# A GNN and LSTM kernel on one core: the first layer's split reordered, one DRAM tensor per tile of gate inputs, an early activation, and the fc weight one tile sooner

## The chip, the cores and the metric

The kernel runs on one core of a Trainium2 chip. Five engines work side by side: TensorE (PE, with its weight loads PEld), VectorE (DVE), ScalarE (ACT), GpSimd (POOL) and SyncE (SP), which here only issues transfers. Each takes its own instructions in order and waits on semaphores for the others. The metric is the device time of one execution, in microseconds; lower is better. Three runs of the kernel before gave 1154.37, 1154.40 and 1155.09 us, median 1154.4.

## What is computed

`x` is 1250 x 512 float32. First comes a graph network on the layer norm of x, then an LSTM over the 1250 rows as one sequence, each added to its input:

```
h    = layernorm(x) @ fc_w.T + fc_b
norm = clip(degree(dst), 1) ** -0.5
layer(v, l): agg = segment_sum((v * norm)[src], dst) * norm
             f, f0 = 0.9 * agg, 0.1 * h
             relu((1-b)*f + b*(f @ w1) + (1-b)*f0 + b*(f0 @ w2) + bias)    b = log(1/l + 1)
x2  = x + layer(layer(h, 1), 2)
out = x2 + lstm(layernorm(x2))     # gates f, i, o: sigmoid; candidate: tanh; hidden size 512
```

There are 20000 edges.

## The kernel before

The rows are cut into 10 tiles (T) of 128 rows. Tile t holds steps 4t to 4t+3 of each of 32 stretches (P) of 40 steps (LEN), because the LSTM is later run on all 32 stretches at once, each started 90 steps early (WARM), instead of one row after the other. A test at the end compares neighbouring stretches and falls back to one row at a time (L862) if they are apart.

**Start (L273 to L486).** Loads are issued on SyncE's queue in program order: source nodes, two tiles of x (`load_rows(0, 2, xt)`, two transfers a tile), the fc weight (L291), tiles 2 and 3, the fc bias (L295), tiles 4 to 9 in eight transfers (L125), then the two w2 weights and two biases. VectorE turns the edges into one-hot rows (`make_onehot`, L373 and L375) and computes layer norm statistics (`stats`, L152) and scales (`scales`, with a square root on ScalarE, L88). ScalarE applies them (`normed`, L401). PE multiplies one-hots into the adjacency `adj` (L389), and the normed tiles with the fc weight into `h` (L175, added at L460), and `h` with the two w2 weights (L175), which VectorE adds to the bias as `base` (`add_base`, L440). In this part the order on PE, VectorE and ScalarE is written out by hand (`manual_schedule`, L310): each of the three runs its instructions as the program lists them, in 13 slots (L442).

**The split.** The aggregation is done in bf16 with each value as a sum of three bf16 planes. For each tile `split_first` does: ScalarE writes plane 0 as h times norm in bf16 (L251), VectorE writes the remainder (`rest`, L253, two buffers), ScalarE rounds it to plane 1 (L256), VectorE writes what is left as plane 2 (L259). Tiles go in the order 6, 7, 8, 9, 0, 1, 2, 3, 4, 5. Three are split in slot 10, three in slot 11, four after the last slot, and after them come the adds of tiles 8 and 9.

**The branch (L897).** The number of edges that are missing from `adj` (L227) is read by every engine, and `fast` or `general` is taken. With these inputs it is `fast`. There the order of instructions is chosen by the planner, which sees what each one waits for, and not by the program's order; an instruction inside the branch stays inside.

**The layers (L703).** PE aggregates for four blocks of 128 features (L722): for each tile k in the order above, three planes times three groups of columns, nine matmuls. Then come products with w1 (L175), and VectorE and ScalarE finish the layer; at the end of the second, `rstd_of` (L88 again) scales groups of tiles.

**The gate inputs (L888).** For each tile PE multiplies with the input weights (L550), VectorE and ScalarE split the sum into three planes (`put_planes`, L765 and L236 to L239), and SyncE stores them to the DRAM tensor `xp_d` (L893). Early steps of the first stretch are zeroed by one transfer from POOL (L752).

**The LSTM (L796).** 130 steps. SyncE loads a step's planes (L771, five buffers), PE adds them into PSUM (L572) and multiplies the state with the weights (L580), then a chain of ScalarE and VectorE forms the new state (L587 to L598). PE, VectorE and ScalarE are hand-ordered again (L827).

Of the kernel before, what the change touches and what calls it, by code (L numbers as in the profile page):

```python
# [38 lines left out]
def gnn_lstm_kernel(  # L39
# [23 lines left out]
    nc = tc.nc  # L63
# [49 lines left out]
    def load_rows(i0, i1, dst):  # L113


        for p0, p1 in ((0, 16), (16, P - 1)):
            if i1 - i0 <= 4:
                for i in range(i0, i1):
                    nc.sync.dma_start(
                        dst[4 * p0:4 * p1, i, :],  # L120
                        bass.AP(tensor=x.tensor, offset=x.offset + (LEN * p0 + 4 * i) * D,
                                ap=[[LEN * D, p1 - p0], [D, 4], [1, D]]))
            else:
                for q in range(4):
                    nc.sync.dma_start(  # L125
                        dst[4 * p0 + q:4 * p1:4, i0:i1, :],
                        bass.AP(tensor=x.tensor, offset=x.offset + (LEN * p0 + 4 * i0 + q) * D,
                                ap=[[LEN * D, p1 - p0], [4 * D, i1 - i0], [1, D]]))
# [66 lines left out]
    with ExitStack() as gnn_stack:  # L195
# [48 lines left out]
        def split_first(pool, tiles):  # L244

            rest = {}
            for n in range(len(tiles) + 1):
                if n < len(tiles):
                    t = tiles[n]
                    rest[t] = pool.tile([R, D], F32, name="rest")  # L250
                    nc.scalar.activation(planes[:, t, 0, :], h[:, t, :], AF.Copy,  # L251
                                         scale=norm[:, t:t + 1])
                    nc.vector.scalar_tensor_tensor(rest[t], h[:, t, :], norm[:, t:t + 1],  # L253
                                                   planes[:, t, 0, :],
                                                   op0=OP.mult, op1=OP.subtract)
                    nc.scalar.copy(planes[:, t, 1, :], rest[t])  # L256
                if n:
                    t = tiles[n - 1]
                    nc.vector.tensor_sub(planes[:, t, 2, :], rest[t], planes[:, t, 1, :])  # L259


# [11 lines left out]
        with tc.tile_pool(name="prep", bufs=1) as prep, \  # L273
# [12 lines left out]
            xt = base1  # L286

            load_last_rows(xt, nc.scalar, fill=True)
            load_rows(0, 2, xt)
            fcw = prep.tile([128, KD, D], F32, name="fcw")  # L290
            nc.sync.dma_start(fcw, fc_w.rearrange("(a p) i -> p a i", p=128))  # L291
            biases = [prep.tile([R, D], F32, name=name) for name in ("fcb", "b1", "b2")]
            fcb, *bl = biases
            load_rows(2, 4, xt)
            nc.sync.dma_start(fcb, row_bcast(fc_b, R))  # L295
            load_rows(4, T, xt)
            w2 = []
# [12 lines left out]
            with tc.manual_schedule(engines={mybir.EngineType.PE, mybir.EngineType.DVE,  # L310
# [6 lines left out]
                def stats(t0, t1):  # L317
                    for t in range(t0, t1):
                        layernorm_stats(work, mv, t, xt[:, t, :])
# [24 lines left out]
                def neg_floor_div(v, n, name):  # L344
# [9 lines left out]
                    return q, r  # L354

                np_src, o_src = neg_floor_div(e_src, LEN, "stretch")
                stats(0, 2)
                na_src, q_src = neg_floor_div(o_src, 4, "tile")
                nc.vector.scalar_tensor_tensor(low, np_src, -4.0, q_src, op0=OP.mult, op1=OP.add)
                nc.vector.scalar_tensor_tensor(key, e_dst, float(T), na_src,  # L360
                                               op0=OP.mult, op1=OP.subtract)
                scales(0, 2)

# [78 lines left out]
                for s in range(T + 3):  # L442
                    c0, c1, c2 = per_slot[s] if s < len(per_slot) else (0, 0, 0)
                    if s < T:
                        xTs[s] = transposed(work, psT, xns.pop(s), "xT")
                    if s < 3:
                        t0, t1 = ((2, 4), (4, 7), (7, T))[s]
                        stats(t0, t1)
                        scales(t0, t1)
                    normed(s + 1)  # L450
                    if 0 <= s - 4 < T - 3:
                        add_base(s - 4)
                    count(c0)
                    if 0 <= s - 1 < T:
                        ps_h[s - 1] = product(psM, xTs.pop(s - 1), fcT)
                    count(c1)
                    if 0 <= s - 2 < T:
                        hTs[s - 2] = transposed(prep2, psT, h[:, s - 2, :], "hT")
                    if 0 <= s - 1 < T:
                        nc.vector.tensor_add(h[:, s - 1, :], ps_h.pop(s - 1), fcb)  # L460
                    count(c2)
                    if s == 2:
                        for l in range(2):
                            with_identity(w2[l], ALPHA * betas[l], ALPHA * (1.0 - betas[l]))
                    if 0 <= s - 3 < T:


                        hT = hTs.pop(s - 3)
                        ps, name = (psM, "psM") if s < T + 1 else (acc, "acc")
                        if s == T + 1:  # L470
                            total(psT.tile([128, KD, R], F32, name="psT")[:1, 0, :1])
                            split_first(prep2, order[3:6])
                        ps_b[s - 3] = [product(ps, hT, w2[0], name)]
                        if s == T:
                            most_edges()
                            count_edges(psT.tile([128, KD, R], F32, name="psT")[:, 0, :])
                            row_totals()
                            degree_norm(prep)
                        ps_b[s - 3].append(product(ps, hT, w2[1], name))
                        if s == T:  # L480
                            add_base(T - 3)
                            split_first(prep2, order[:3])
                split_first(prep2, order[6:])
                add_base(T - 2)
                add_base(T - 1)
                assert counted == n_batch and not blocks  # L486
        n_missing = nc.values_load(missing, min_val=0, max_val=E + R)

# [2 lines left out]
        xw_d = dram.tile([P * LEN, 4 * G], F32, name="xw_d")  # L491


        xp_d = dram.tile([LEN, EARLY + P, 3, 4 * G], BF16, name="xp_d")
        x2_d = dram.tile([P * LEN, D], F32, name="x2_d")

        def in_time(v, i):
# [245 lines left out]

        def tile_steps(i):

            return bass.AP(tensor=xp_d.tensor,
                           offset=xp_d.offset + (4 * i * (EARLY + P) + EARLY) * 12 * G,
                           ap=[[12 * G, P], [(EARLY + P) * 12 * G, 4], [1, 12 * G]])

        def zero_steps(rows):  # L750

            nc.gpsimd.dma_start(  # L752
                bass.AP(tensor=xp_d.tensor, offset=xp_d.offset,
                        ap=[[(EARLY + P) * 12 * G, LEN], [12 * G, EARLY], [1, 12 * G]]), rows)


        v_bufs = adj.rearrange("b a i r -> b (a i r)")[:, :8 * G].bitcast(F32).rearrange(
            "b (n g) -> b n g", g=G)
        zeros = adj.rearrange("b a i r -> b (a i r)")[:EARLY * LEN, 8 * G:20 * G]
        pl_bufs = planes.rearrange("b t i d -> b (t i d)")[:, :24 * G].rearrange(  # L760
            "b (n i g) -> b n i g", n=2, i=3)

# [5 lines left out]
        def open_step(load, ps_g, n):  # L768

            xs = load.tile([3 * P, 4, NG, 128], BF16, name="xs")  # L770
            nc.sync.dma_start(  # L771
                xs.rearrange("r j g m -> r (j g m)"),
                bass.AP(tensor=xp_d.tensor,
                        offset=xp_d.offset + (n % LEN * (EARLY + P) + EARLY + n // LEN) * 12 * G,
                        ap=[[4 * G, 3 * P], [1, 4 * G]]))
            return open_gates(ps_g, lambda j: sel, lambda j, s: xs[:, j, :, 64 * s:64 * (s + 1)])

# [18 lines left out]
        def lstm(late, Wh):  # L796
# [6 lines left out]
            with tc.tile_pool(name="state", bufs=2) as state, \  # L803
# [22 lines left out]
                stores = [8, 16, 24, 32, 38, LEN]  # L826
                with tc.manual_schedule(engines={mybir.EngineType.PE, mybir.EngineType.DVE,  # L827
                                                 mybir.EngineType.Activation}):
                    hT = [state.tile([128, 2, 32], F32, name=f"hT{s}") for s in range(2)]
                    for s in range(2):  # L830
                        nc.vector.memset(cgs[s], 0.0)
                        nc.vector.memset(hT[s], 0.0)
                    for n in range(-WARM, LEN):
                        if n == 0:
                            keep_state(snap, hT)
                        ps = open_step(load, ps_g, n)
                        add_gates(ps, hT, Wh)
# [93 lines left out]
```

## Time and profile before

| what | value |
|---|---|
| median of three runs | 1154.4 us |
| the profiled execution, its own time | 1152.8 us |
| its span | 1151.0 us |
| PE busy | 1024.6 us, 89% |
| VectorE busy | 518.4 us, 45% |
| ScalarE busy | 344.9 us, 30% |
| POOL busy | 65.7 us, 6% |
| first aggregation matmul starts at | 200.4 us |
| first LSTM step starts at | 550.2 us |

The profile is of one execution. Start times are counted from the span's start. A line such as `L722 PE` means the instructions that line 722 issued on PE; `SPq` is the queue of transfers that SyncE issues. "Issue" is time in which an engine waited for nothing that the profile shows. PEclk is the share of PE's full clock that was granted.

### The profile page before, as it was taken

How to read it: one execution, taken by the hardware profiler on the slowest of the kernel's cores; microseconds unless marked ns; L12 is line 12 of the kernel's file. 1: busy time of each engine (PE TensorE's matmuls, PEld its weight loads, DVE VectorE, ACT ScalarE, POOL GpSimd, SP SyncE). 2: the span in 40 equal slices, each digit the busy share in tenths (PEclk: the TensorE clock that was granted, in tenths of full speed). 3: DMA queues.
4: the chain of work that ended last, by engine and by line, in shares of the span. 5: the costliest groups of instructions: out<-in, count | busy, mean ns of one | idle time of the engine just before them, and what ended most of it. 6: DMA issues, size and time to landing. Idle time of an engine off the chain costs nothing.

```text
span 1151.0 us, 27480 instructions
## 1 busy us (share of the span) xinstructions
PE 1024.6 (89%) x11340; PEld 535.8 (47%) x11356; DVE 518.4 (45%) x1775; ACT 344.9 (30%) x1286; POOL 65.7 (6%) x117
## 2 busy tenths in 40 slices
PE   5999996999999999999788888888888888888884
PEld 3455552554455444444444444444444444444442
DVE  7876566003300765555344434444444434434433
ACT  2321125103300033333333333333333333333332
POOL 0000000300002270000000000000000000100111
PEclk9999998999999999999999999999999999999998
DMA  8000001700200273222632222323232232333331
GB/s 233 2 1 1 1 1 58 202 1 18 72 1 1 102 222 130 110 110 110 193 97 86 90 92 86 96 84 98 85 95 87 89 93 84 105 101 97 108 83 20
DMA packets 42363, 96.22 MB, mean 84 GB/s; under 512 B 6062, under 2 KB 21783, under 8 KB 40825
## 3 DMA queue, kind: packets, MB, share of 16 engines
q1 hardware_dynamic: 38464, 83.98, 23.5%
q0 software_dynamic: 3440, 10.16, 2.8%
q8 instruction: 92, 1.51, 0.5%
q14 instruction: 46, 0.38, 0.1%
q10 hardware_dynamic: 321, 0.19, 0.1%
HBM read 71.93 MB, written 19.76 MB: 80 GB/s over the span
## 4 chain that ended last, share of the span: by engine, by line
PE 65%; DVE 17%; ACT 10%; issue 4%; DMA 2%; SPq 1%; DVEq 0%; ACTq 0%
PE gates L580 28%; PE psM L175 13%; PE agg L722 11%; PE psM L550 10%; DVE pr L593 3%; ACT th L596 3%; DVE hT L598 3%; DVE hh L597 3%; DVE cg L594 3%; ACT cg L587 3%; ACT sg L589 2%; PE acc L389 2%; DVE od L375 1%; DVE ob L373 1%; DMA fcw<-in_L_gnn_fc_w_dram 1%
## 5 line engine op out<-in xcount | busy, mean ns | idle before, releaser
L580 PE MATMUL gates<-Wh,hT 128*32 128x256 f32 x8320 | 482.5, 383 | 75.5 <-DVE hT L598 75.5
L580 PEld LDWEIGHTS gates<-Wh,hT 128*32 128x32 f32 x8320 | 245.5, 110 | 286.4 <-DVE hT L598 152.1
L593 DVE TENSOR_TENSOR pr<-sg,cg 128x128 f32<-128x128 f32 x260 | 70.5, 271 | 223.7 <-ACT sg L589 223.5
L722 PE MATMUL agg<-adj,planes 128*128 128x512 bf16 (+1 forms) x704 | 131.6, 347 | 10.8 <-DVE x L440 9.8
L550 PE MATMUL psM<-Wx,xT 128*128 128x512 f32 x320 | 138.7, 594 | 1.5 <-ACT xT L169 1.2
L587 ACT ACTIVATE cg<-gates 128x64 f32<-128x64 f32 x260 | 58.0, 223 | 248.9 <-PE gates L580 244.8
L596 ACT ACTIVATE th<-cg 128x64 f32<-128x64 f32 x260 | 66.6, 256 | 138.8 <-DVE cg L594 138.8
L722 PEld LDWEIGHTS <-planes 128*128 128x128 bf16 x720 | 71.1, 99 | 72.2 <-DVE x L440 10.6
L597 DVE TENSOR_TENSOR hh<-so,th 128x64 f32<-128x64 f32 x260 | 58.6, 225 | 86.4 <-ACT th L596 86.4
L550 PEld LDWEIGHTS psM<-Wx,xT 128*128 128x128 f32 x320 | 60.5, 190 | 76.7 <-issue 72.8
L598 DVE STREAM_TRANSPOSE hT<-hh 128x64 f32<-128x64 f32 x260 | 63.8, 245 | 28.3 <-DVE hh L597 1.4
L589 ACT ACTIVATE sg<-gates 128x128 f32<-128x128 f32 x260 | 70.8, 272 | 0.2
L594 DVE TENSOR_TENSOR cg<-pr 128x64 f32<-128x64 f32 x260 | 58.5, 225 | 8.9
L591 ACT ACTIVATE so<-gates 128x64 f32<-128x64 f32 x260 | 60.2, 232 | 0.0
L843 POOL TENSOR_TENSOR base<-base,hh 128x128 f32<-128x128 f32 x40 | 18.2, 455 | 694.6 <-issue 534.9
L175 PE MATMUL psM<-w,hT 128*128 128x512 f32 x128 | 56.9, 596 | 0.0
L572 PE MATMUL gates<-xs,sel 96*32 96x256 bf16 x1040 | 52.5, 273 | 4.0 <-DMA xs<-xp_d 4.0
L375 DVE TENSOR_SCALAR od<-ids,key 125x820 f16<-125x820 f16 (+42 forms) x160 | 55.5, 347 | 0.0
L389 PE MATMUL acc<-od,ob 125*128 125x400 f16 (+22 forms) x360 | 47.8, 259 | 4.5 <-DVE od L375 3.0
L373 DVE TENSOR_SCALAR ob<-ids,low 125x128 f16<-125x128 f16 x160 | 39.5, 247 | 17.1 <-PE acc L389 16.9
L572 PEld LDWEIGHTS <-sel 96*32 96x32 bf16 x1040 | 30.6, 98 | 28.6 <-issue 4.8
L389 PEld LDWEIGHTS <-ob 125*128 125x128 f16 x360 | 29.5, 97 | 26.8 <-issue 10.8
(152 smaller groups left out, 675.0 us busy)
## 6 DMA issues: line engine op xcount, KB each, us to landing
xs<-xp_d SPq DMA_DIRECT2D x130, 384.0 KB, 3.2
xp_d<-planes SPq DMA_DIRECT2D x10, 1536.0 KB, 5.5
w<-in_L_gnn_w_dram SPq DMA_DIRECT2D x2, 1024.0 KB
w<-in_L_gnn_w_dram POOLq DMA_DIRECT2D x2, 1024.0 KB, 7.2
xp_d<-adj POOLq DMA_DIRECT2D x1, 1440.0 KB, 7.8
h<-in_x_dram SPq DMA_DIRECT2D x10, 128.0 KB, 2.7
base<-x SPq DMA_DIRECT2D x20, 64.0 KB, 2.2
base<-x POOLq DMA_DIRECT2D x20, 64.0 KB, 2.3
```

The source lines that it names most:

```text
L175: nc.tensor.matmul(p, lT[:, k, :], rhs[:, k, :], start=(k == 0), stop=(k == KD - 1))
L389: nc.tensor.matmul(blocks[i][:, (d0 - i * BW) * T:(d1 - i * BW) * T], ob, od[:, (d0 - lo) * T:(d1 - lo) * T], start=False, stop=last)
L550: nc.tensor.matmul(p, yT[:, k, :], Wx[:, k, j, :, :], start=(k == 0), stop=(k == KD - 1))
L580: nc.tensor.matmul(ps[s][32 * j:32 * (j + 1), :, :], hT[b // 2][:, b % 2, :], Wh[:, b, j, :, 64 * s:64 * (s + 1)], start=False, stop=(b == 3))
L587: nc.scalar.activation(cg[:, 1, :], p[:, 3, :], AF.Tanh)
L589: nc.scalar.activation(sg, p[:, 0:2, :], AF.Sigmoid)
L593: nc.vector.tensor_mul(pr, sg, cg)
L594: nc.vector.tensor_add(cg[:, 0, :], pr[:, 0, :], pr[:, 1, :])
L596: nc.scalar.activation(th, cg[:, 0, :], AF.Tanh)
L597: nc.vector.tensor_mul(hh[:, m], so, th)
L598: nc.vector.transpose(hT.rearrange("p b c -> p (b c)"), hh[:, m])
L722: nc.tensor.matmul(p[:, :n * R], planes[:, k, pl, f * 128:(f + 1) * 128], adj[:, k, t0:t0 + n, :].rearrange("b i r -> b (i r)"), start=(k ...
```

## The change

- `split_first` issues a tile's second ScalarE step (L256) after the next tile's first step on both engines, not ahead of it.
- Four tiles are split in slot 11 instead of three. In slot 12 the add of tile 8 and the split of tiles 3 and 4 come ahead of the last product in program order; then come the add of tile 9 and the split of tile 5.
- `xp_d` becomes ten DRAM tensors, one per tile of gate inputs. The zeroing becomes ten transfers of 12 rows each.
- One row tile is loaded ahead of the fc weight instead of two, and statistics and scales are grouped as 0, 1 to 3, 4 to 6, 7 to 9. The scales of tile 0 come ahead of the one-hot keys.
- An activation with Sigmoid on a constant column stands first in the LSTM's hand-ordered part.

```diff
-                    nc.scalar.copy(planes[:, t, 1, :], rest[t])
                 if n:
                     t = tiles[n - 1]
+                    nc.scalar.copy(planes[:, t, 1, :], rest[t])
                     nc.vector.tensor_sub(planes[:, t, 2, :], rest[t], planes[:, t, 1, :])
...
-            load_rows(0, 2, xt)
+            load_rows(0, 1, xt)
             fcw = prep.tile([128, KD, D], F32, name="fcw")
             nc.sync.dma_start(fcw, fc_w.rearrange("(a p) i -> p a i", p=128))
...
-            load_rows(2, 4, xt)
+            load_rows(1, 4, xt)
...
-                stats(0, 2)
+                stats(0, 1)
+                scales(0, 1)
...
-                scales(0, 2)
...
-                        t0, t1 = ((2, 4), (4, 7), (7, T))[s]
+                        t0, t1 = ((1, 4), (4, 7), (7, T))[s]
...
                             total(psT.tile([128, KD, R], F32, name="psT")[:1, 0, :1])
-                            split_first(prep2, order[3:6])
+                            split_first(prep2, order[3:7])
+                        if s == T + 2:
+                            add_base(T - 2)
+                            split_first(prep2, order[7:9])
...
-                split_first(prep2, order[6:])
-                add_base(T - 2)
                 add_base(T - 1)
+                split_first(prep2, order[9:])
...
-        xp_d = dram.tile([LEN, EARLY + P, 3, 4 * G], BF16, name="xp_d")
+        xp_d = [dram.tile([4, EARLY + P, 3, 4 * G], BF16, name=f"xp_d{i}") for i in range(T)]
...
-            nc.gpsimd.dma_start(
-                bass.AP(tensor=xp_d.tensor, offset=xp_d.offset,
-                        ap=[[(EARLY + P) * 12 * G, LEN], [12 * G, EARLY], [1, 12 * G]]), rows)
+            for i in range(T):
+                nc.gpsimd.dma_start(
+                    bass.AP(tensor=xp_d[i].tensor, offset=xp_d[i].offset,
+                            ap=[[(EARLY + P) * 12 * G, 4], [12 * G, EARLY], [1, 12 * G]]), rows)
...
-        zeros = adj.rearrange("b a i r -> b (a i r)")[:EARLY * LEN, 8 * G:20 * G]
+        zeros = adj.rearrange("b a i r -> b (a i r)")[:4 * EARLY, 8 * G:20 * G]
...
+            steps = xp_d[n % LEN // 4]
...
+                    nc.scalar.activation(warm, ones, AF.Sigmoid)
                     hT = [state.tile([128, 2, 32], F32, name=f"hT{s}") for s in range(2)]
```

More of the change, by code (lines that the diff above doesn't have):

```diff
@@ L744, in tile_steps @@
         def tile_steps(i):
-            return bass.AP(tensor=xp_d.tensor,
-                           offset=xp_d.offset + (4 * i * (EARLY + P) + EARLY) * 12 * G,
+            return bass.AP(tensor=xp_d[i].tensor, offset=xp_d[i].offset + EARLY * 12 * G,
                            ap=[[12 * G, P], [(EARLY + P) * 12 * G, 4], [1, 12 * G]])
         def zero_steps(rows):
-            nc.gpsimd.dma_start(
-                bass.AP(tensor=xp_d.tensor, offset=xp_d.offset,
-                        ap=[[(EARLY + P) * 12 * G, LEN], [12 * G, EARLY], [1, 12 * G]]), rows)
+            for i in range(T):
+                nc.gpsimd.dma_start(
+                    bass.AP(tensor=xp_d[i].tensor, offset=xp_d[i].offset,
+                            ap=[[(EARLY + P) * 12 * G, 4], [12 * G, EARLY], [1, 12 * G]]), rows)
         v_bufs = adj.rearrange("b a i r -> b (a i r)")[:, :8 * G].bitcast(F32).rearrange(
             "b (n g) -> b n g", g=G)
-        zeros = adj.rearrange("b a i r -> b (a i r)")[:EARLY * LEN, 8 * G:20 * G]
+        zeros = adj.rearrange("b a i r -> b (a i r)")[:4 * EARLY, 8 * G:20 * G]
         pl_bufs = planes.rearrange("b t i d -> b (t i d)")[:, :24 * G].rearrange(
@@ L770, in open_step @@
             xs = load.tile([3 * P, 4, NG, 128], BF16, name="xs")
+            steps = xp_d[n % LEN // 4]
             nc.sync.dma_start(
                 xs.rearrange("r j g m -> r (j g m)"),
-                bass.AP(tensor=xp_d.tensor,
-                        offset=xp_d.offset + (n % LEN * (EARLY + P) + EARLY + n // LEN) * 12 * G,
+                bass.AP(tensor=steps.tensor,
+                        offset=steps.offset + (n % 4 * (EARLY + P) + EARLY + n // LEN) * 12 * G,
                         ap=[[4 * G, 3 * P], [1, 4 * G]]))
```

## The prediction

> **What bounds the kernel now.** I read the page first (PE busy 89%, the chain 65% on PE), then the chain of waits in order of time, looking for the places where PE is not what carries it. There are three: the first 38 us, where VectorE and the loads carry it; the stretch 176 to 200 us, where the first layer's split does; and the first LSTM step. The chain in the second stretch (start, us, what):
>
> ```profile
> 188.33 0.62 ACT planes L256
> 188.95 0.63 ACT planes L251
> 189.59 0.02 issue
> 189.61 0.76 DVE rest L253
> 190.37 0.02 issue
> 190.40 0.62 ACT planes L256
> ...
> 199.71 0.61 DVE x L440
> 200.32 0.05 issue
> 200.37 0.61 PE agg L722
> 200.98 0.22 issue
> 201.19 11.15 PE agg L722 x49
> 212.34 0.05 issue
> 212.39 9.14 PE agg L722 x50
> ```
>
> Two things are to be seen. One tile of the split costs a full round trip, ScalarE L251, VectorE L253, ScalarE L256, one after the other: 190.40 - 188.33 = 2.07 us a tile, and the idle rows agree (VectorE waits 0.7 to 1.3 us for L251, ScalarE 0.82 us for L253). And the first aggregation matmul starts 0.05 us after the last base add (L440), while PE's own last product ended at 190.62: it waits 9.76 us. Afterwards 50 matmuls take 11.97 us where the next 50 take 9.19 with the issue gap. The table by stretches says why (span, PE, PEld, DVE, ACT, POOL busy, PEclk, DMA share, GB/s):
>
> ```profile
> 195.00:200.30 5.30, 0.00 (x0) 0.00 (x0) 4.51 (x8) 2.05 (x4) 0.00 (x0) 0.54 0.08 25
> 200.30:205.70 5.40, 5.11 (x15) 2.27 (x17) 0.91 (x5) 1.23 (x1) 4.72 (x7) 0.50 1.01 283
> 205.70:211.00 5.30, 5.30 (x31) 2.84 (x30) 0.00 (x0) 1.62 (x1) 2.42 (x4) 1.00 1.01 317
> ```
>
> The clock was granted at half while PE stood still, and stayed there for 5.3 us after it resumed.
>
> **The split (hand-ordered, so the order holds).** Removed: the ScalarE round trip. L251 of the next tile now comes ahead of L256 of this one, so both engines stay fed. Costs, as intervals from start to start of neighbours: L251 0.63, L256 0.53, so ScalarE needs 1.16 a tile; L253 0.67 (187.55 to the L259 at 188.22), L259 and L440 0.60 (the L440 pair 198.44, 199.03), so VectorE needs 1.27. VectorE sets the pace: 2.07 becomes about 1.27. From a result to the start of its user: L251 to L253 0.76, L253 to L256 0.79, L256 to L259 0.65 us after the producer's start.
>
> The end is not ten tiles times 0.8, because the adds moved too. What PE waits for is the last L440 of tile 9, and ahead of that now stand nine tiles, not ten. On VectorE from 176.77 (first L253, unchanged, since it waits behind the add of tile 7): nine L253 6.03, nine L259 5.40, L227 0.1, three L440 1.80, together 13.3. Walking both queues instruction by instruction leaves 1.2 us of waits, most at tile 9, whose L251 queues on ScalarE behind the copy of hT. So the last L440 starts at 191.28, ends 191.97, and PE starts at 192.02: **-8.35 us**. From below PE itself limits it: its product ends at 190.62, plus one L440 0.69 and two hops gives 191.4. From above, twice the waits give 193.2. Tile 5 is split after that, done about 194.0; the aggregation takes it last, nine tiles of nine matmuls at 0.183 us later (206.8), so 12.8 us of cover; without it, PE would start at 194.06.
>
> PE's branch (L897) is no new limit: its sequencer's records show the compare and branch from 183.7 to 187.1, while products ran, and they hang on L227, which now comes no later.
>
> **The clock.** PE's idle shrinks from 9.76 to 1.4 us. The nearest row is the LSTM, where PE waits in every step, up to 1.8 us, and the stretch from 600 to 900 us shows a granted clock of 1.00:
>
> ```profile
> PE gates L580 <- DVE hT L598: 75.5, 129, 1.8
> ```
>
> So I take full clock: 11.97 - 9.19 = **-2.8 us**. At the other end, if the gate closes anyway, 0. The Trainium skill, "TensorE: Matmul & The Clock Gate", section "What's actually happening", puts the gate on a free-running window of about 3.4 us. By it 1.4 us is safe whatever the phase, and 3.4 us of idle is the edge: that decides between my forecast and the second rival.
>
> **Loads at the start.** Two row loads move from ahead of the fc weight to behind it; statistics of tile 1 move behind the first one-hots. VectorE's work is the same; the order changes which wait it meets. SyncE's own waits show (us in total, times, longest):
>
> ```profile
> SPq L125 <- DMA fcw<-in_L_gnn_fc_w_dram: 3.6, 1, 3.6
> ```
>
> and, by its timeline,
>
> ```profile
> 12.49 6.21 SPq L125 DMA_DIRECT2D base<-in_x_dram  x8
> ```
>
> The loads of tiles 4 to 9 sit 3.6 us behind the landing of the fc weight: eight completion signals are used in turn, and the first L125 takes the one that the weight holds. The statistics of tile 4 then wait for those rows until 22.97 and VectorE is the chain to 38. The weight is now issued two row loads sooner, 4.56 - 1.68 = 2.88, and its own 7.9 us shrink by about 0.85 (one less 256 KB bias in flight at some 300 KB/us; the stretch from 20 to 28 us moved 335 GB/s), so it lands at about 10.3. But counted out, the transfer eight behind it is now a half of tile 3, not L125: queued behind that are the other half, the bias and L125, 0.6 + 0.9 + 0.55 us, so L125 goes out at about 12.4 instead of 12.49: **-0.1 us**. If the signal falls on L125 itself, L125 moves 1.7 and VectorE, which reaches those statistics at about 21.5 (one pair of statistics fewer ahead of the one-hots, less waiting for L88), gains 1.4. If the weight lands a microsecond later than I reckon, +0.9. The fc weight's transposes on PE come earlier, which nobody waits for. A cold window of PE at 38.4 to 41.8 (one product 5.2 us, not 3.5) may move by its phase: 1.7 either way, taken as 0.
>
> **The table load.** The first LSTM step shows
>
> ```profile
> 554.51 0.22 ACT L587 ACTIVATE cg<-gates 128x64 f32<-128x64 f32 x1 [4.27 <-PE gates L580]
> 554.75 1.28 ACT L589 ACT_TABLE_LOAD   x1
> 556.04 0.28 ACT L589 ACTIVATE sg<-gates 128x128 f32<-128x128 f32 x1
> ```
>
> The second load lies on the chain: 1.3 us to be had if Sigmoid's set (in which Tanh then runs without a load, as the rest of the LSTM shows) is there before. But the added activation reads only constants. The planner issues what is ready: the LSTM's x loads (L821) run at 382 to 438 us, ahead of the stores of L893, and the memsets of L831 run ahead of an older L237. So I expect it at the front of the branch, near 194 us, where ScalarE idles. Then the Sqrt of L88 needs its set back and the LSTM still loads twice: **0 us**. This is where a rule speaks against the change: "ScalarE: Activation LUTs", "Table sets: the hidden batching unit", asks for calls grouped by set, and this call breaks a group of Sqrts. Its price by row is one load of 1.28 at L88 (383.71). VectorE's L530 behind it ends at 385.59, and PE wants that buffer at about 387.95, so 2.36 us of cover hide it. By the page's section "What ACT_TABLE_LOAD costs", 2.66 a switch, 0.3 would show. I take the row: the load at 554.75 and its user at 556.04 leave no room for more than 1.3.
>
> **One tensor per tile.** Stores and step loads keep their bytes and shapes. They do not wait for each other now either: two step loads go out at 546.88, before the last store at 549.69. What opens them is the last L765 (ends 546.85), which the change leaves alone: 0. The zeroing is ten POOL transfers, not one: at 0.75 (L515's spacing) they end at 380.4 instead of 373.5, and POOL's next work is at 392.82, so 12 us of cover; the memset before keeps 6144 elements a partition.
>
> **Sum.** On the profiled execution: 1152.8 (span 1151.0, 1.8 around it) - 8.35 - 2.8 - 0.1 = 1141.5. The median lies 1.6 above that execution, so the prediction is **1154.4 - 11.3 = 1143.1**.
>
> **Rivals.** (a) PE waits for all of VectorE's early work, tile 5's split too. In the old order the last L440 was both the last PSUM reader and the last VectorE instruction, so the trace cannot part them; against it, SyncE's Wx loads left at 198.09, before the adds were done, so waits are by buffer. PE starts at 194.06 (-6.3), idle 3.4: cold gives 1148.1, warm 1145.3. Chance 0.12. (b) The start or the table load pays (-1.4, -1.3): 1140.4 to 1141.8; chance 0.10. (c) It does not do what it says: the waits between the engines only move, and less than 2.3 us is left, 1152.5; against it, the 0.8 us idle before each L256 is real and the next L251 needs nothing. Chance 0.03. (d) Slower: with ten tensors, step loads land too late. Steps are 4.5 us apart (first and last L572: 582 us over 129), five buffers give 18 us; a landing now takes 3.2, at most 10.2. It bites from 18 us on, and 18.6 (+0.15 a step, +19 us) would give 1162. Nothing in the trace points there; with what I overlook, 0.05. My forecast has 0.70.
>
> **Range and chances.** About 0.2% (2.3 us) is what a measurement of this kernel can tell. The range runs from (b) to (a) cold, 1140.4 to 1148.3; outside are (c), (d) and slips, some 0.13. Faster: 0.70 + 0.12 + 0.10 = 0.92; same 0.03; slower 0.05.
>
> **What would show it.** First L722 near 192.0 right behind an L440, with L259 of tile 5 after it; clock 1.00 in the following 10 us and 50 matmuls in 9.2; a table load near 194 and again at L88, both LSTM loads still there; statistics of tile 4 near 22.9. I am wrong if L722 follows an L259, if the clock drops, or if the LSTM's steps are no longer 4.5 us apart.

## The result, and the profile after

The changed kernel takes **1145.2 us** (median of four runs, 1143.5 to 1145.7) beside 1154.4 for the kernel before on the same chip: ratio 0.9921, 95% interval 0.9903 to 0.9938. The prediction was 1143.1, range 1140.4 to 1148.3. The direction, the size and the place were right; the sum was 2 us too favourable, and the section on why the prediction was right says where those 2 us lie.

The profiled execution took 1143.5 us (span 1141.7), against 1152.8 (1151.0). First the chain of waits of the changed kernel around the start of the aggregation (start, us, what):

```profile
185.35 0.76 DVE rest L253
186.12 0.02 issue
186.14 0.63 ACT planes L258
...
190.02 0.79 DVE planes L259 x2
190.81 0.48 issue
191.29 0.68 DVE base L440
191.98 0.61 DVE x L440
192.59 0.05 issue
192.63 0.39 PE agg L724
193.03 0.05 issue
193.08 8.93 PE agg L724 x49
```

The string of ScalarE and VectorE taking turns is gone: two `rest` and two `planes` instructions now follow each other on VectorE, as its timeline below shows. PE starts 0.05 us after the last base add, at 192.63 instead of 200.37, and 49 matmuls now take 8.93 us where they took 11.15. That PE waits for the add and not for tile 5's split is seen there too (VectorE of the changed kernel):

```profile
188.60 1.41 DVE L253 SCALAR_TENSOR_TENSOR rest<-h,norms,planes 128x512 f32<-128x512 f32 x2
190.02 1.35 DVE L259 TENSOR_TENSOR planes<-rest,planes 128x512 bf16<-128x512 f32 x2
191.29 0.68 DVE L440 TENSOR_TENSOR base<-acc,b 128x512 f32<-128x512 f32 x1
191.90 0.68 DVE L440 TENSOR_TENSOR x<-acc,b 128x512 f32<-128x512 f32 x1
192.49 0.74 DVE L253 SCALAR_TENSOR_TENSOR rest<-h,norms,planes 128x512 f32<-128x512 f32 x1
193.92 0.69 DVE L259 TENSOR_TENSOR planes<-rest,planes 128x512 bf16<-128x512 f32 x1 [0.68 <-ACT planes L258]
```

Tile 5's last plane starts 1.3 us after PE did. The table by stretches of the changed kernel (span, PE, PEld, DVE, ACT, POOL busy, PEclk, DMA share, GB/s) shows the full clock on both sides of the start:

```profile
190.60:192.60 2.00, 0.14 (x1) 0.00 (x0) 2.00 (x5) 0.68 (x2) 0.00 (x0) 1.00 0.86 348
192.60:198.00 5.40, 5.31 (x29) 2.90 (x31) 1.33 (x2) 1.25 (x2) 3.41 (x5) 1.00 0.53 187
```

SyncE's wait for the fc weight is still there, on another line (its waits, then its timeline):

```profile
SPq L119 <- DMA fcw<-in_L_gnn_fc_w_dram: 3.4, 1, 3.4
```

```profile
11.70 0.55 SPq L295 DMA_DIRECT2D fcb<-in_L_gnn_fc_b_dram  x1
12.30 6.21 SPq L125 DMA_DIRECT2D base<-in_x_dram  x8
```

And ScalarE loads the Sigmoid table early, loads the Sqrt table again, and then loads both tables in the first LSTM step as before (ScalarE's timeline, cut to what concerns tables):

```profile
197.36 1.28 ACT L833 ACT_TABLE_LOAD   x1 [3.48 <-issue]
198.66 0.20 ACT L833 ACTIVATE warm<-ones 128x1 f32<-128x1 f32 x1
...
358.02 1.28 ACT L88 ACT_TABLE_LOAD   x1
...
538.62 1.28 ACT L589 ACT_TABLE_LOAD   x1
544.29 0.22 ACT L589 ACTIVATE cg<-gates 128x64 f32<-128x64 f32 x1 [4.39 <-PE gates L582]
544.53 1.28 ACT L591 ACT_TABLE_LOAD   x1
545.83 0.28 ACT L591 ACTIVATE sg<-gates 128x128 f32<-128x128 f32 x1
```

All the experiments are read in the same six stretches, taken from the instruction records of one profiled execution each; the medians come from more than one chip. "Rows in" is the start of VectorE's statistics of tile 4 (it waits there for the loads). From there to the first L251 every kernel takes 151.4 to 151.7 us, so a spread in the first column goes straight to the end. "50 matmuls" is the time of the first 50 that the trace holds. Four traces hold all 720 matmul records of the aggregation (84 transposes, late table load, four remainders, bias later), the others 704, so 9.09 there and 9.42 here are the same speed.

| kernel | median us | rows in | L251 to aggregation | 50 matmuls | aggregation to first gate matmul | gate to state of step 0 | last state to end |
|---|---|---|---|---|---|---|---|
| before | 1154.4 | 22.97 | 25.76 | 12.02 | 349.80 | 8.57 | 12.30 |
| after | 1145.2 | 23.08 | 17.90 | 9.42 | 347.32 | 8.58 | 13.22 |
| split and adds alone | 1143.1 | 23.20 | 17.89 | 9.42 | 347.45 | 8.31 | 12.30 |
| adds alone | 1152.2 | 22.66 | 25.37 | 11.51 | 349.51 | 8.29 | 12.30 |
| L256 deferred alone | 1146.2 | 22.13 | 19.49 | 11.10 | 349.27 | 8.29 | 12.30 |
| one tensor | 1144.4 | 24.74 | 17.90 | 9.42 | 347.45 | 8.47 | 12.30 |
| 84 transposes | 1156.2 | 23.67 | 29.82 | 11.39 | 349.86 | 8.32 | 12.30 |
| 20 products | 1158.9 | 22.62 | 34.92 | 9.79 | 347.72 | 9.19 | 12.30 |
| late table load | 1143.4 | 23.31 | 17.89 | 9.10 | 347.41 | 8.43 | 13.22 |
| four remainders | 1144.6 | 23.90 | 17.36 | 9.09 | 347.47 | 8.26 | 13.23 |
| zeroing on SyncE | 1144.5 | 23.68 | 19.59 | 9.42 | 347.26 | 8.31 | 12.20 |
| bias later | 1144.3 | 22.81 | 19.58 | 9.09 | 347.69 | 8.55 | 13.22 |
| PE kept busy | 1142.3 | 24.40 | 17.88 | 9.42 | 348.43 | 5.53 | 13.22 |
| all together | 1141.9 | 24.01 | 17.35 | 9.42 | 348.43 | 5.53 | 12.30 |

The 129 later LSTM steps take 579.4 to 580.6 us in every kernel. Between the two profiled executions the sum is 0.12 (start) - 7.86 (split) - 2.48 (aggregation to gate) - 0.02 (steps) + 0.93 (end) = -9.3 us, which is their difference, 1152.8 to 1143.5.

### The profile page after: what moved, and what is told of

Same layout as the page of the kernel before. It is cut to its first block, busy times and chain, and to the rows that moved or that the text cites. A ratio compares the mean times of both kernels' runs of the same rounds, so it can differ in the third digit from the quotient of the medians.

```text
span 1141.7 us, 27486 instructions
## 1 busy us (share of the span) xinstructions
PE 1022.1 (90%) x11340; PEld 535.5 (47%) x11356; DVE 518.4 (45%) x1775; ACT 347.5 (30%) x1289; POOL 70.9 (6%) x126
## 3 DMA queue, kind: packets, MB, share of 16 engines
q0 software_dynamic: 3872, 10.16, 3.8%
## 4 chain that ended last, share of the span: by engine, by line
PE 66%; DVE 17%; ACT 9%; issue 4%; DMA 1%; SPq 1%; DVEq 0%; ACTq 0%
PE gates L582 28%; PE psM L175 13%; PE agg L724 11%; PE psM L552 10%; DVE pr L595 3%; ACT th L598 3%; DVE hT L600 3%; DVE hh L599 3%; DVE cg L596 3%; ACT cg L589 3%; ACT sg L591 2%; PE acc L389 2%; DVE od L375 1%; DVE ob L373 1%; DMA fcw<-in_L_gnn_fc_w_dram 1%
## 5 line engine op out<-in xcount | busy, mean ns | idle before, releaser
L724 PE MATMUL agg<-adj,planes 128*128 128x512 bf16 (+1 forms) x704 | 129.1, 343 | 2.7 <-DVE x L440 1.9
L236 ACT CAST planes<-adj 128x512 bf16<-128x512 f32 x40 | 24.7, 618 | 57.4 <-DVE adj L767 53.3
```

The costliest lines, as they stand in the source:

```text
L724: nc.tensor.matmul(p[:, :n * R], planes[:, k, pl, f * 128:(f + 1) * 128], adj[:, k, t0:t0 + n, :].rearrange("b i r -> b (i r)"), start=(k ...
```

## Experiments

The experiments ran on three chips. Ratios below are to the kernel before on the same chip, where its median was 1153.95, 1153.3 or 1153.5 us.

**The split and the adds, alone and apart.** The first kernel has only these two edits on the kernel before, the second only the order of tiles and adds, the third only the deferred L256:

```diff
-                    nc.scalar.copy(planes[:, t, 1, :], rest[t])
                 if n:
                     t = tiles[n - 1]
+                    nc.scalar.copy(planes[:, t, 1, :], rest[t])
...
-                            split_first(prep2, order[3:6])
+                            split_first(prep2, order[3:7])
+                        if s == T + 2:
+                            add_base(T - 2)
+                            split_first(prep2, order[7:9])
...
-                split_first(prep2, order[6:])
-                add_base(T - 2)
                 add_base(T - 1)
+                split_first(prep2, order[9:])
```

> Only the split and the adds are changed, against the kernel before. Theory (split and clock carry all of it, loads and table load nothing, the ten POOL transfers cost about 0.9 us at the end of the program): the first aggregation matmul starts about 7.7 us earlier (192.6), clock 1.00 after it, so 10.3 us in all at that point and at the end: span about 1140.7, 0.9 below the changed kernel. Rival (the loads or the tensors carry part of the gain): less than 9 us.

> Only the order of splits and adds (four, two, one tiles with the adds between), L256 left ahead of the next tile. Theory: a tile still costs 2.07 us; only tile 5's split and the two adds of tile 8 leave the end, so the last L440 ends near 197.5 and PE starts there, 2.5 to 3 us earlier; PE has idled 7 us, so the clock is at half again and nothing more is gained: -2.5 to -3. Rival (the adds in between are what matters): more than half of the 9.3.

> Only L256 is put behind the next tile's first step, the groups and adds as before. Theory: VectorE sets the pace at about 1.3 us a tile; ten tiles and four adds end near 194.5, so PE starts 5.9 us earlier. Its idle is then 3.9 us, over the 3.4 us of a clock window, so the clock decides: -5.9 if it falls to half, -8.6 if not. Rival (PE waits for the last VectorE instruction, not for the last PSUM reader): the same start here; it is told apart by L440 or L259 ahead of the first matmul in the other run.

Measured: both 1143.1 us, ratio 0.9905 (0.9889 to 0.9922); adds alone 1152.2, 0.9982 (0.9973 to 0.9990); deferral alone 1146.2, 0.9928 (0.9912 to 0.9945). The two edits together do all that the change does to the aggregation's start, 17.89 against 17.90 us. The deferral carries it: 6.3 of the 7.9 us. The adds alone gave less than expected in this profile, 0.4 us, but there PE's product of tile 7 ran at half clock (5.38 us instead of 3.68), which is 1.7 us on the path. This half rate comes and goes with the old order and with the new (last section); without it the adds would give about 2.1, an estimate. The deferral alone leaves 3.49 us of idle PE. Its table by stretches:

```profile
187.00:192.90 5.90, 2.52 (x6) 0.76 (x4) 5.71 (x9) 2.03 (x4) 0.16 (x1) 1.00 0.67 210
193.00:197.00 4.00, 3.93 (x12) 1.78 (x14) 0.90 (x4) 1.91 (x1) 3.38 (x5) 0.58 0.74 221
197.00:202.00 5.00, 5.00 (x29) 2.69 (x28) 0.00 (x0) 0.00 (x0) 2.56 (x4) 1.00 0.91 296
```

One stretch at half clock follows, 193.62 to 197.04 by the clock records, where 7.68 us of idle in the kernel with the adds alone brought two (196.87 to 203.70). So the adds are worth more than their own microseconds: they bring the idle from 3.5 to 1.9 us, and with that the last half-rate stretch goes.

**Is it the idle that brings the half clock?** Two kernels fill PE's pause in the kernel before with work whose result is not used, 84 transposes or 20 products, ahead of the branch:

```diff
                 split_first(prep2, order[6:])
+                for _ in range(21):
+                    p = psT.tile([128, KD, R], F32, name="psT")
+                    for k in range(KD):
+                        nc.tensor.transpose(p[:, k, :], ident, ident)
                 add_base(T - 2)
```

```diff
                 split_first(prep2, order[6:])
+                for _ in range(5):
+                    p = psT.tile([128, KD, R], F32, name="psT")
+                    for k in range(KD):
+                        nc.tensor.matmul(p.rearrange("p k r -> p (k r)"), hT[:, k, :],
+                                         w2[1][:, k, :], start=(k == 0), stop=(k == KD - 1))
                 add_base(T - 2)
```

> The kernel before with 84 transposes of the identity on PE behind its last early product, into a PSUM tile that nothing reads; they fill the 9.8 us in which it stood still. Theory (the clock had fallen because PE was idle, and that alone made the first 50 aggregation matmuls slow): the first matmul starts where it did (25.8 us after the first L251), the clock stays at 1.00, 50 matmuls take 9.4 instead of 12.0 us, so 2.6 us less in all. Rival (they are slow for another reason, the transfers of w and Wx that run beside them): still 12.0, and nothing gained.

> The kernel before, with twenty products of 128x512 (0.43 us each, result unused) on TensorE ahead of the branch, so that TensorE computes until about 199 us where it stood still from 190.6. Theory (the half clock comes from TensorE standing still for 9.8 us): the aggregation starts as before, 25.8 us after the first L251, idle falls to 1 to 2 us, the clock stays 1.00 and the first 50 matmuls take 9.4 us instead of 12.0: 2.6 us shorter, about 1150.8. Rival (the start of the aggregation itself, with the DMA queues at full load, brings the half clock): still 12.0 us, same time as before. If the compare and branch again runs late, as behind the 84 small transposes, the aggregation starts up to 4.7 us later.

The transposes missed their aim: 1156.2 us, ratio 1.0030 (1.0023 to 1.0036). Chain of waits:

```profile
199.16 0.69 DVE x L440
199.85 0.49 issue
...
203.20 1.96 issue
205.16 11.02 PE agg L726 x47
```

The adds are done at 199.85, yet PE starts at 205.16. Its sequencer's records say why: the read of the missing-edge count starts at 199.70 and the compare and branch runs from 200.28 for 4.81 us. In the kernel before, the branch ran at 183.70 to 187.1, while PE computed products until 190.62. With the 84 small instructions ahead of it, it was taken when they were nearly through (the last one starts at 200.24). PE then idled 4.65 us and the clock was halved again (203.03 to 209.85), so this run does not show what an aggregation without the pause does.

The products are longer and fewer, and the branch is hidden behind them:

```profile
191.68 17.18 PE psT L487 x40
208.87 0.04 issue
208.91 0.38 PE agg L727
```

Its table by stretches after the start, in the same columns as before:

```profile
208.80:214.20 5.40, 5.06 (x28) 2.67 (x28) 0.90 (x4) 1.91 (x1) 4.70 (x7) 1.00 0.66 178
```

I had sized them wrongly: the records count two matmuls of 0.43 us for each float32 product, so they took 17.2 us, not 8.6, and the kernel is slower, 1158.9 us, 1.0046 (1.0029 to 1.0063). But the clock is read from the stretch after: with 0.06 us of idle the records show 1.00 throughout, the 50 matmuls take 9.79 us instead of 12.02, and the way from the start of the aggregation to the first gate matmul is 347.72 us instead of 349.80. So the aggregation's own start does not halve the clock; the pause does. Full DMA queues, the other rival, are only at a share of 0.66 here. The kernel before rules them out by itself: its clock falls at 195.45, five microseconds ahead of the aggregation, and is back at 1.00 from 205.7 on with the share at 1.01.

**One tensor again.** The changed kernel with `xp_d` as one tensor and one zeroing transfer:

```diff
-        xp_d = [dram.tile([4, EARLY + P, 3, 4 * G], BF16, name=f"xp_d{i}") for i in range(T)]
+        xp_d = dram.tile([LEN, EARLY + P, 3, 4 * G], BF16, name="xp_d")
...
-            for i in range(T):
-                nc.gpsimd.dma_start(
-                    bass.AP(tensor=xp_d[i].tensor, offset=xp_d[i].offset,
-                            ap=[[(EARLY + P) * 12 * G, 4], [12 * G, EARLY], [1, 12 * G]]), rows)
+            nc.gpsimd.dma_start(
+                bass.AP(tensor=xp_d.tensor, offset=xp_d.offset,
+                        ap=[[(EARLY + P) * 12 * G, LEN], [12 * G, EARLY], [1, 12 * G]]), rows)
```

and the changed kernel with the ten tensors kept and their zeroing on SyncE's queue:

```diff
             for i in range(T):
-                nc.gpsimd.dma_start(
+                nc.sync.dma_start(
```

> The changed kernel with one DRAM tensor again and so one zeroing transfer. Theory: the stages are the same to 0.1 us, and what comes after the last step (POOL's drain, 6.4 us with ten transfers against 5.7 with one) is 0.9 us shorter: span about 1140.8 against 1141.7. Rival (the tensors help the step loads): slower than the changed kernel by 1 us or more, at the first LSTM step.

> The changed kernel with its ten zeroing transfers on SyncE's queue instead of POOL's; the ten tensors stay. Theory (the 0.9 us more at the end of the program come from the number of transfers that POOL issues): POOL's semaphore step and drain go back from 1.75 and 6.43 us to about 1.57 and 5.70 us, all else as in the changed kernel, about 1144.4. Rival (the ten tensors cost it): they stay at 6.4.

Measured: 1144.4 us, 0.9916 (0.9899 to 0.9933), and 1144.5 us, 0.9924 (0.9908 to 0.9941). The end of the program is what they were for. POOL's last two long instructions, after the last step, by its records:

| kernel | zeroing transfers from POOL | semaphore step us | drain us | last state to end us |
|---|---|---|---|---|
| zeroing on SyncE | 0 | 1.552 | 5.616 | 12.20 |
| before; one tensor | 1 | 1.572 | 5.697 | 12.30, 12.30 |
| after | 10 | 1.751 | 6.432 | 13.22 |

That is 0.10 us for each zeroing transfer that POOL has issued, although it issued them more than 700 us before. It is paid at the very end, where the other engines wait for POOL. The tensors themselves cost nothing that a stage shows. With the zeroing on SyncE the median is the expected one, though in its profile a half-rate stretch (174.29 to 177.70) fell on the product of tile 7 and took 1.7 us. With one tensor the profiled span is 1142.9 us, not the expected 1140.8, mainly because the rows came in at 24.74.

**The table load.** The changed kernel with the early Sigmoid reading a value that exists only after the last L88, so that it can't be issued early:

```diff
-                    nc.scalar.activation(warm, ones, AF.Sigmoid)
+                    nc.scalar.activation(warm, rstd2[:, 5:6], AF.Sigmoid)
```

> The changed kernel with the added activation reading a column of the last group's scales instead of a constant, so that it can't be issued before the last Sqrt. Theory (it was issued at the branch's front and undone by L88): three table loads in all instead of five, none in the LSTM; the step's sigmoid follows the tanh by 0.1 us, not 1.3, and the first step ends 1.3 us earlier: 1.3 us less than the changed kernel. Rival (the step waits for PE's second half anyway): under 0.3 us.

Measured: 1143.4 us, 0.9916 (0.9898 to 0.9934). Only two table loads are left (I had counted three), at 1.2 and 394.8, and none in the LSTM. Yet the state of step 0 comes 8.43 us after the first gate matmul instead of 8.58, which is what the rival said. The table by stretches of that step:

```profile
539.00:542.60 3.60, 2.62 (x32) 1.45 (x36) 0.26 (x1) 0.00 (x0) 0.00 (x0) 0.53 0.97 363
542.60:546.00 3.40, 3.40 (x40) 1.64 (x36) 0.52 (x2) 0.57 (x4) 0.00 (x0) 0.50 0.95 283
546.00:552.00 6.00, 5.05 (x100) 2.72 (x96) 2.62 (x12) 2.24 (x12) 0.00 (x0) 1.00 1.03 259
```

Here the half clock lasted 6.8 us, two stretches, where the changed kernel's profile has one (540.30 to 543.71). PE was late, and the 1.3 us had nobody waiting for them. What the load is worth with one stretch at half clock was not measured. PE stands still ahead of that step too, 4.2 us, so the next kernel treats both.

**PE kept busy ahead of the LSTM.** On top of the late table load, 18 small products on PE, whose result is not used:

```diff
+                    junk = ps_c.tile([128, 128], F32, name="junk")
+                    for _ in range(18):
+                        nc.tensor.matmul(junk, ident, cgs[0].rearrange("p a m -> p (a m)"),
+                                         start=True, stop=True)
```

> The changed kernel with the early Sigmoid reading a value that is there only after L88 (as in the run with the late table load), and with eighteen small products (result unused) on TensorE between the last product of the gate inputs (535.8) and the first gate matmul (539.94). Theory (TensorE's 4.2 us of idle there bring the half clock of the LSTM's first step): clock 1.00 in that step, the first cell starts 1.9 us sooner after the first gate matmul and meets no table load, 1.3 us: hT of step 0 about 3.2 us sooner, 545.3, about 1142.0. Rival (small products do not hold the clock, or the half clock there has another cause): hT of step 0 at 548.4 as with the late table load alone, about 1144.

Measured: 1142.3 us, 0.9904 (0.9887 to 0.9920). Chain of waits:

```profile
537.91 4.26 PE junk L840 x36
542.17 0.33 PE gates L574 x8
542.50 2.21 PE gates L582 x40
...
544.74 0.23 ACT cg L589
544.96 0.18 ACT sg L591
```

No table load stands between the two activations, the clock record is 1.00 from 42.5 us to the end of the LSTM, and the state of step 0 comes 5.53 us after the first gate matmul instead of 8.58: 3.05 us, close to the 3.2 expected. But the products were again twice as many as I counted (36 records, 4.26 us), and the first gate matmul stood behind them: 348.43 instead of 347.32 us after the aggregation began. Of 3.05 us, 1.1 went there. By 0.118 us a record, twelve products would end in time, an estimate; that was not run.

**Four remainder buffers.** The changed kernel with two more buffers for `rest`:

```diff
-                    rest[t] = pool.tile([R, D], F32, name="rest")
+                    rest[t] = (pool.tile([R, D], F32, name="rest") if order.index(t) % 2
+                               else work.tile([R, D], F32, name="xn"))
```

> The changed kernel with four buffers for the remainder instead of two. Theory (the 0.6 us that the split took over the reckoning are waits of L253 for the L259 just ahead of it, which still reads the buffer: 0.80 from start to start instead of 0.60): from the first L251 to the first aggregation matmul 17.3 us instead of 17.9. Rival (those waits are ScalarE's): 17.9 as before.

Measured: 1144.6 us, 0.9925 (0.9907 to 0.9942); the way from L251 to the aggregation is 17.36 us instead of 17.90. On VectorE, the changed kernel with two buffers:

```profile
178.32 0.69 DVE L259 TENSOR_TENSOR planes<-rest,planes 128x512 bf16<-128x512 f32 x1
179.12 0.75 DVE L253 SCALAR_TENSOR_TENSOR rest<-h,norms,planes 128x512 f32<-128x512 f32 x1
```

and with four:

```profile
179.16 0.69 DVE L260 TENSOR_TENSOR planes<-xn,planes 128x512 bf16<-128x512 f32 x1
179.79 0.75 DVE L254 SCALAR_TENSOR_TENSOR xn<-h,norms,planes 128x512 f32<-128x512 f32 x1
```

From one start to the next 0.80 us become 0.63. With two buffers the remainder that L253 writes is the one that the L259 just ahead reads, and VectorE waits for its own end.

**The loads at the start.** The changed kernel with the fc bias loaded after tiles 4 to 9:

```diff
-            nc.sync.dma_start(fcb, row_bcast(fc_b, R))
             load_rows(4, T, xt)
+            nc.sync.dma_start(fcb, row_bcast(fc_b, R))
```

> The changed kernel with the fc bias loaded behind the rows of tiles 4 to 9 instead of ahead of them. Theory (after the fc weight's landing SyncE's queue sets when those rows go out, and the rows set when VectorE goes on): L125 starts 0.55 us earlier, the statistics of tile 4 too, and the first L251 0.5 us earlier, up to the clock windows' phase of about 1.5 us. Rival (VectorE or PE is behind anyway): statistics where they were.

Measured: 1144.3 us, 0.9918 (0.9900 to 0.9937). L125 starts at 12.31, as in the changed kernel. Chain of waits:

```profile
3.01 7.50 DMA fcw<-in_L_gnn_fc_w_dram
10.53 0.86 SPq L119
...
11.43 0.84 SPq L119
...
12.31 0.61 SPq L125
```

From the landing of the weight to L125 it is 1.78 us instead of 2.39, the 0.6 expected. The landing was 0.6 later in this execution (7.50 us in flight, 6.89 in the changed kernel's), and that hid it; the next section compares the landing over all profiles. The 19.58 us ahead of the aggregation in the table hold a half-rate stretch (172.96 to 176.37) on the product of tile 7, as with the zeroing on SyncE.

**All together.** One tensor, four remainders, late table load, 18 products:

> The changed kernel with all that the other runs point to: one DRAM tensor and one zeroing transfer (0.9 us at the end), four remainder buffers in the split (0.55 us before the aggregation), the late table load and the eighteen small products ahead of the LSTM (3.2 us): 4.6 us shorter than the changed kernel, about 1140.6. If the parts stand in each other's way, less: where only the first two pay, 1143.7.

Measured: 1141.9 us, 0.9901 (0.9884 to 0.9917), the lowest median here. By stages the parts keep their worth, 17.35, 348.43, 5.53 and 12.30 us: -0.55 + 1.11 - 3.05 - 0.93 = -3.4 us against the changed kernel. The 1.1 us missing from the expected 4.6 are the products' excess. The two ratios, 0.9901 and 0.9921, are only 2.3 us apart, and so are the two profiled spans (2.4), where the rows came in 0.9 us later with all together. The intervals of the ratios overlap, so it is the stages, not the ratio alone, that say it is faster.

## Why the prediction was right, and where it was off

**Split and adds, -8.35 us: right mechanism, 0.5 too much.** Measured -7.86 from the first L251. The walk through both queues held in its order; the failed term is "L259 and L440 0.60": the step from L259 to the next L253 is 0.80, because of the shared remainder buffer, and there are three such steps ahead of the last add. The run with four buffers gets 0.54 us back and so shows it. PE's idle was 1.90 us instead of 1.4 for the same reason.

**Loads at the start, -0.1 us: wrong.** In the one profile the first L251 moved by +0.12, which looks like a hit, but over all profiles it isn't one. Start of the first L125, which the landing of the fc weight and the issues behind it set:

| order of loads | profiles | first L125 at us | mean | rows in, mean |
|---|---|---|---|---|
| before's | 6 | 12.49, 11.75, 12.26, 11.69, 12.78, 11.73 | 12.12 | 22.88 |
| the change's | 7 | 12.30, 13.74, 12.74, 13.26, 13.14, 13.58, 13.39 | 13.17 | 23.87 |

The change's load order costs about **1.0 us**. Of this, 0.83 is fixed by the issues, if the weight takes as long to land in both orders: 3.00 + 2.39 - 4.56. The rest is the difference of the mean flights, which is less than their scatter. Three terms of the working failed. The weight's flight was to shrink by 0.85 us; it is 7.55 us on average before (7.12 to 8.22) and 7.77 after (6.91 to 8.35), as one can see by taking the issue (4.56 and 3.00) from the start of the transfer that waits for it. "0.6 + 0.9 + 0.55" behind it is 2.39, not 2.05, since the first of these transfers takes 0.86 to issue and they stand 0.05 apart. And the landing was added up wrongly: 2.88 + 7.92 - 0.85 is 9.95, not 10.3. In the one profile the last two cancel (9.91 + 2.39 = 12.30 beside the 12.4 that was forecast), which is luck. The profile of before, 12.49, was also one of its later ones. The working had named this case ("if the weight lands a microsecond later than I reckon, +0.9") and kept it off the sum. The counting of signals was right in kind: SyncE waits at a half of a row tile (L119), tile 2 and not tile 3, and no longer at L125.

**The clock, -2.8 us: right.** Measured -2.6 over the first 50 matmuls and -2.48 over the whole way to the gate. (The forecast took 9.19 from later matmuls; the first 50 records take 9.42 at full clock.) The edge that the prediction drew from the Trainium skill, "TensorE: Matmul & The Clock Gate", section "What's actually happening", was tested: 1.4 to 1.9 us of idle left the clock at 1.00 in all nine profiles that have both edits, 3.49 us halved it for one stretch, 7.68 us for two. Within a trace all changes of the clock lie multiples of 3.41 us apart, which agrees with the page's free-running window. But 3.4 us of idle is not the edge. Counted by windows of that grid over the pauses ahead of the aggregation and of the first LSTM step, the full clock was lost after windows with 2.35 us of idle or more (four remainders: 538.06 to 541.47), and held after those with 1.96 or less. A pause of 3.49 us lost the clock though the window that ended with the fall still held 0.56 us of work (190.21 to 193.62). Here the measurement decides: in these traces a pause was safe whatever its phase up to about 2 us, not up to 3.4.

**The table load, 0 us: right.** The load moved to 197.36 (194 was forecast), ahead of work that nobody waits for, the Sqrt table came back, and both loads of the LSTM stayed. Only the place of the second was wrong: not at the Sqrt itself, under 2.36 us of cover, but at 358.02, 15 us ahead of it. On the chain a load takes 1.28 us and its user starts 1.30 us after the load does (544.53, 545.83), as the prediction took it; the 2.66 that it quotes from the Trainium skill's "ScalarE: Activation LUTs", section "What ACT_TABLE_LOAD costs", does not show at any load of this trace.

**Ten tensors, 0 us: wrong by 0.9.** The steps are 4.46 us apart as before, so rival (d) is dead. The transfers were covered where they are issued, though eight went out at once (362.51 to 367.25) and two only at 414.36. What the prediction left out is that POOL pays for them once more after the last step. Its sum is made of the stages up to the last state; the 12.3 us of the span behind it got no row.

**The rivals.** (a) fell: PE follows the last L440, and L259 of tile 5 comes after it. (b), that the start or the table load would pay, fell, and the start went the other way. (c) fell with the 7.86 us.

**The sum.** -11.3 was predicted for this pair of executions and -9.3 measured: 0.49 of the split, 0.32 of the clock, 0.22 of the start, 0.93 of the end. Against average executions the start's share is about 1.0. The two together are about the 2.1 us by which the median of the split and the adds alone lies below that of the whole change. By the ratios to the kernel before it is 1.8 us, and their intervals overlap, so this is no proof.

## What to carry to other kernels

A software pipeline of two engines is set by its slower engine only if its buffers are as many as its stages in flight: count the buffers together with the instructions, and price the interval between the two neighbours that share one. Price the end of the program too, where each of POOL's zeroing transfers came back as 0.10 us that nothing covers. And take the landing of a load from several executions: one profile had it a microsecond off, in the direction of the forecast.

## What was not expected of the hardware

- POOL's closing step and drain grow with the number of transfers it issued, 0.10 us for each (7.17, 7.27 and 8.18 us with 0, 1 and 10 zeroing transfers). Packets and bytes are not what counts: POOL's queue has 3232, 3440 and 3872 packets in these three. So one transfer with 208 packets adds 0.10 us and ten with 640 together add 1.01, three times as much for a packet, while the bytes of the one and of the ten are the same. POOL issues 68 other transfers; if each costs the same, they make up 6.9 of the 7.17 us, an estimate that no run tested.
- The compare and branch on PE took 3.3 to 4.4 us behind long products and 4.8 us behind the short ones. It was hidden in the first case, because it was taken while PE still had six to seven microseconds of products to run, and not in the second. What sets its length is open.
- Removing a table load of 1.28 us from the chain gave 0.15 us in an execution where PE was at half clock for two stretches there, and with the clock held the two together gave 3.05.
- The clock was halved for one stretch around 173 to 176 us in 4 of the 14 profiles, with the old order of the split and with the new, where PE's records show no pause. Ahead of it stand twenty products one column wide (L213; 169.7 to 172.0 in the kernel with the adds alone). It costs 1.7 us when it falls on the product of tile 7, as the same stretch of two kernels shows, the adds alone first and the changed kernel second:

```profile
172.90:176.40 3.50, 3.50 (x6) 1.46 (x5) 1.67 (x7) 0.76 (x2) 0.00 (x0) 0.51 0.02 5
172.90:176.40 3.50, 3.50 (x11) 1.59 (x10) 2.20 (x12) 1.55 (x3) 0.00 (x0) 1.00 0.02 5
```

The windows of 3.41 us part the 14 traces without exception. In the four, 2.16 to 2.29 us of the narrow products' 2.29 lie inside one window, and the clock falls at that window's end. In the ten others a window's edge cuts them, so that at most 2.11 us lie in one window, and the clock holds. The margin is thin, but it lies where the edge of real pauses lies (between 1.96 and 2.35 us), so such products seem to count as idle, although the profile shows PE busy. No run varied them on purpose.
